# Taking the second chunk's edge counts in the lead-in, and moving list pieces behind the first chunk's norm

## The chip, the cores and the metric

The kernel runs as one program on one core of a Trainium2 chip. The metric is the device time of one execution in microseconds (us); with one core, the slowest core is that core. The engines are called by the names that the profile uses: PE (TensorE, matrix products), DVE (VectorE), ACT (ScalarE), POOL (GpSimd) and SP (SyncE, which only issues DMA transfers here). Each engine works through its own instructions in order.

## The reference, cut to what matters

Two layers run over 4096 tokens of width 256. In layer 0 a graph convolution is followed by a Mamba block and a mixture of experts; in layer 1 a second graph propagation, which keeps the 700 largest entries of each row, is followed by another mixture of experts.

```python
# layer 0, graph part, on x normalised
h = relu(adj @ x @ gcn_w + gcn_b)
h = layernorm(h) * ln_g + ln_b
... mamba(h): u = silu(conv(h @ w_in)); dt = softplus(...); scan over the 4096 tokens
# layer 1, graph part, on x normalised
sim  = tanh(adj * adj)
filt = sim * (adj > 0)
vals, idx = top_k(filt, 700)          # of each row
new_adj = filt with only these entries kept
feat = relu(new_adj @ (tanh(h @ W_proj + b_proj) @ W_gcn) + b_gcn)
```

The adjacency has few entries per row. If no row has more than 700 positive entries, the top-700 keeps everything, and `new_adj` is `filt`. The kernel counts the positive entries of each row to know that; were a row to have more, a branch at the end would compute the layer again.

## The kernel before, in words

The 4096 tokens are cut into 8 chunks of 512 (`CW`). Each chunk is a half-open range of rows of the adjacency; the kernel reads the transposed adjacency in tiles.

**The first propagation** (`propagation`, from L854) multiplies the adjacency with the normalised x. One chunk has two halves of 256 rows (`HW`), and one half has 8 tiles `at` (128 partitions x 4 x 256, 512 KB each, a pool of 3 buffers, loaded by SP at L795). A tile is used up in 4 pieces; one piece is one `yield` of the generator and two products at L871 (four records in the profile). After 32 pieces the half is copied out of PSUM by ACT (L877, tile `pts`), and a 33rd `yield` follows. Pieces are interleaved by hand with other work: `advance(k)` issues k of them. For chunk 0 the propagation is called with `count=True`: DVE then also adds up, tile by tile, which entries are positive (L864 for the first tile of a half, L866 for the others), into a bf16 tile `cnt`, which PE sums over partitions (L882) and DVE reduces to the largest row count (L886, L888, into `cmax`).

In what follows the 8 tiles of the first half of chunk 1 are called t0 to t7, and those of its second half s0 to s7.

**The lead-in** is what happens before the scan of chunk 0 can begin: chunk 0's propagation, then the steps 9 to 31 of `Front(0)`: bias and relu (L948, L952), statistics (L956 to L961), normalisation (`do_normal`, L964 on DVE and L968 on ACT), turning (L976), the in-projection (L999), convolution (L1016), `u`, `dt`, and the softplus of `dt` (`do_soft`, L1081 to L1089, in steps 28 to 31). Between these, the table `FILL` says how many pieces of chunk 1's propagation follow each step: 8 behind step 11, and so on up to all that are left for the lead-in behind step 26. The last 15 of the 66 pieces are issued in steps 0, 1, 2, 4 and 6 of the scan of chunk 0.

**Lists.** The rows of chunks 2, 4 and 6 are turned into lists of neighbours (`Lists.pair`, from L543), 128 rows pairwise at a time, so 6 pairs, of which 2 are done in the lead-in. One pair is 12 pieces on DVE: 8 that each scan a loaded 512 KB tile for the 8 largest of each segment (L577, L578; loads at L566), one that makes keys (L587 to L598), two that select (L606, L608), and one that finishes (L612 to L637). Before the change, 8 pieces run within the second half of chunk 0's propagation, the other 4 of the first pair directly behind chunk 0's last products, and all 12 of the second pair behind step 11.

**The scan** is 8 chunks of 32 steps. In each step DVE scans (two of L1377) and multiplies (L1387), ACT makes the decays (L1370), POOL makes the inputs (L1354) and starts an accumulating transfer (L1391). PE, DVE, ACT and POOL work in the order written by hand here; SP's order is left to the scheduler.

**The second propagation** (L1896 on) runs over the dense chunks 0, 1, 3, 5 and 7, 16 steps k of two blocks each. For each k, ACT makes tanh of the square of a tile `at1` (L1846 to L1848, three steps ahead), DVE counts its positive entries unless the chunk is 0 (L1853, L1856), PE multiplies (L1864); at the end of a chunk PE sums the counts (`total`, L1873), and DVE reduces them (L1878) and finishes the rows (`finish`, L1882, L1886). The rows of the listed chunks are gathered meanwhile: POOL starts one indirect transfer per list slot (L1726) into a ring of buffers, and DVE adds each in (L1742), 2.85 slots for each k. The manual order covers SP here too.

Of the kernel before, what the change touches and what calls it, by code (L numbers as in the profile page):

```python
# [10 lines left out]
F32 = mybir.dt.float32  # L11
BF16 = mybir.dt.bfloat16
I32 = mybir.dt.int32
AF = mybir.ActivationFunctionType
ALU = mybir.AluOpType
AX = mybir.AxisListType
# [3 lines left out]
P = 128  # L20
CW = 512
# [20 lines left out]
EARLY_LISTS = 12  # L42
# [4 lines left out]
def kernel(ctx: ExitStack, tc: tile.TileContext, out: bass.AP, **a):  # L47
    nc = tc.nc
# [3 lines left out]
    NT = N // P  # L52
# [730 lines left out]
    with ExitStack() as s1:  # L783
# [70 lines left out]
        def propagation(c, count=False):  # L854


            halves = psts[c] = []
            for r0 in range(c * CW, c * CW + CW, HW):
                pt = ps_pt.tile([P, DB, HW], F32, name="pt", tag="pt")
                for j4 in range(NT // 4):  # L860
                    at = ats.pop(0) if ats else adjacency(r0, j4)
                    if count and j4 == 0:
                        cnt = w2p.tile([P, 4, HW], BF16, name="cnt0", tag="db")
                        nc.vector.tensor_scalar(cnt, at, 0.0, None, ALU.is_gt)  # L864
                    elif count:
                        nc.vector.scalar_tensor_tensor(cnt, at, 0.0, cnt, ALU.is_gt, ALU.add)  # L866
                    for jj in range(4):
                        j = 4 * j4 + jj
                        for k in range(DB):

                            nc.tensor.matmul(  # L871
                                pt[:, k, :], xl[:, j, k * P:(k + 1) * P], at[:, jj, :],
                                start=(j == 0 and k == 0), stop=(j == NT - 1 and k == DB - 1),
                            )
                        yield
                pts = w1p.tile([P, DB, HW], F32, name="pts", bufs=2)
                nc.scalar.copy(pts, pt)  # L877
                halves.append(pts)
                if count:
                    pc = ps_y.tile([P, CW], F32, name="psy", tag="psy")  # L880
                    for jj in range(4):
                        nc.tensor.matmul(  # L882
                            pc[:1, :HW], ones[:, :1], cnt[:, jj, :], start=(jj == 0), stop=(jj == 3)
                        )
                    h = (r0 // HW) % 2
                    nc.vector.tensor_reduce(chalf[:, h:h + 1], pc[:1, :HW], AX.X, ALU.max)  # L886
                    if h == 1:
                        nc.vector.tensor_tensor(  # L888
                            cmax[:, c:c + 1], chalf[:, :1], chalf[:, 1:], ALU.max
                        )  # L890
                yield True
# [438 lines left out]
        class Step:  # L1330
# [64 lines left out]
            def total(self):  # L1395
                f, m = self.f, self.m
                if self.g == 0:
                    f.psy[m] = ps_y.tile([P, CW], F32, name="psy", tag="psy")
                    nc.tensor.matmul(
                        f.psy[m], dD[:, m, :], f.us[:, m, :], start=True, stop=False  # L1400
                    )
                last = 0 if self.paired else 1
                for j in range(last + 1):
                    nc.tensor.matmul(  # L1404
                        f.psy[m], ident, self.hc[:, j, :],
                        start=False, stop=(self.g == GS - 1 and j == last),
                    )
# [7 lines left out]
        with tc.manual_schedule(engines={  # L1415
# [19 lines left out]
            def advance(k=1, wait=False):  # L1435


                while k > 0:
                    k -= 1
                    if next(prop, None) and wait:  # L1440
                        break
                return k
# [41 lines left out]
                next(made)  # L1484
            advance(1)
            fr.do_gcn(1)
            for _ in range(EARLY_LISTS - NT // 4):
                next(made)
            prop, left = propagation(1), 2 * NT + 2 - late
            for i in range(9, STEPS):  # L1490
                fr.at(i, Front.EARLY)
                fr.at(i)
                if i == 11:
                    for _ in made:
                        pass
                k = min(FILL.get(i, 0), left)
                advance(k)
                left -= k
            advance(left)
            steps, tails, kept, gated, summed, owed = [], [], {}, [], 0, 0  # L1500
            for n in range(NC * STEPS):
                c, i = divmod(n, STEPS)
# [84 lines left out]
    with ExitStack() as s2:  # L1587
# [241 lines left out]
        cnts = {}  # L1829
# [12 lines left out]
        def source(k):  # L1842
            c, j2 = seq[k]
            at = ats.pop(k)
            f = ready[k] = wk.tile([P, 2, CW], F32, name="f1", bufs=LEAD + 1)
            nc.scalar.activation(f, at, AF.Relu)  # L1846
            nc.scalar.activation(f, f, AF.Square)
            nc.scalar.activation(f, f, AF.Tanh)  # L1848
            if c == 0:
                pass  # L1850
            elif j2 == 0:
                cnt = cnts[c] = tb.tile([P, 2, CW], BF16, name="cnt", bufs=2)
                nc.vector.tensor_scalar(cnt, at, 0.0, None, ALU.is_gt)  # L1853
            else:
                cnt = cnts[c]
                nc.vector.scalar_tensor_tensor(cnt, at, 0.0, cnt, ALU.is_gt, ALU.add)  # L1856
# [40 lines left out]
        with tc.manual_schedule(engines={  # L1897
            mybir.EngineType.PE, mybir.EngineType.DVE, mybir.EngineType.Activation,
            mybir.EngineType.Pool, mybir.EngineType.SP,
        }):  # L1900
            for k in range(AHEAD):
                fetch(k)
            for k in range(LEAD):
                source(k)
                fetch(k + AHEAD)
            features()
            taken.fetch()
            for k, (c, j2) in enumerate(seq):
                if k == TABLES:
                    table = table()  # L1910
                if j2 == 0:
                    pf = ps_f.tile([P, TPC, D], F32, name="pf")
                if k + LEAD < len(seq):
                    source(k + LEAD)
                if k + LEAD + AHEAD < len(seq):
                    fetch(k + LEAD + AHEAD)
                if ended is not None and k % H2 == 0:
                    finish(*ended)
                    ended = None
                if k in ROUTES:  # L1920
                    b = ROUTES[k]
                    routes[b] = route.prepare(b)
                for b in list(routes):
                    if next(routes[b], routes) is routes:
                        del routes[b]
                if k >= TABLES:
                    next(table, None)
                taken.upto(int(PACE * (k - 2)))
                product(k, pf)
                if j2 == H2 - 1:  # L1930
                    ended = (c, pf, total(c) if c else None)
            finish(*ended)
        assert not routes and taken.done == len(taken.slots)
        for _ in table:
# [239 lines left out]
```

## Time and profile before

| what | value |
|---|---|
| median of 6 runs | 2375.28 us (2367.64 to 2388.14) |
| the profiled execution | 2373.01 us |
| its span, first to last instruction | 2371.2 us |
| granted PE clock, mean | 0.942 |
| PE busy | 2103.5 us, 89% |
| DVE busy | 1812.9 us, 76% |
| ACT busy | 1193.4 us, 50% |
| POOL busy | 1401.2 us, 59% |
| counts of the second propagation (L1856) | 60 of 1.22 us |
| counts of chunk 0 in the first propagation (L866) | 14 of 1.21 us |

The span is that of one execution; 1.8 us of that execution's time lie outside it, and the median of the runs is 2.3 us above it. Busy shares are means over stages with different limits: lead-in 0 to 155 us, scan 155 to 1330 us, first experts up to about 1560 us, features of layer 1 to 1676 us, second propagation to 2069 us, last experts to the end.

In the rows of the timeline the columns are: start and duration in us, engine, line, operation, what it writes and reads, the shape, how many instructions are merged, and in brackets the idle time before it with what ended it. In the rows of windows they are: the window and its length, then each engine's busy time with its number of instructions (PE, its weight loads, DVE, ACT, POOL), the granted PE clock, the DMA engines' share and GB/s.

### The profile page before, as it was taken

How to read it: one execution, taken by the hardware profiler on the slowest of the kernel's cores; microseconds unless marked ns; L12 is line 12 of the kernel's file. 1: busy time of each engine (PE TensorE's matmuls, PEld its weight loads, DVE VectorE, ACT ScalarE, POOL GpSimd, SP SyncE). 2: the span in 40 equal slices, each digit the busy share in tenths (PEclk: the TensorE clock that was granted, in tenths of full speed). 3: DMA queues.
4: the chain of work that ended last, by engine and by line, in shares of the span. 5: the costliest groups of instructions: out<-in, count | busy, mean ns of one | idle time of the engine just before them, and what ended most of it. 6: DMA issues, size and time to landing. Idle time of an engine off the chain costs nothing. (4 is left out here: it accounts for less than half of the span.)

```text
span 2371.2 us, 28092 instructions
## 1 busy us (share of the span) xinstructions
PE 2103.5 (89%) x8235; PEld 1497.6 (63%) x8235; DVE 1812.9 (76%) x3207; ACT 1193.4 (50%) x2064; POOL 1401.2 (59%) x1056
## 2 busy tenths in 40 slices
PE   7899999999999999997896899968679799699884
PEld 6665565656665564654564787845568677577773
DVE  6959999999999999999997895145229799753242
ACT  4146657555665746567662223214368677333221
POOL 1037777787877778776762454420447677745551
PEclk9999999999999999998997999989879899899997
DMA  8559999999989999998975998734355555467794
GB/s 285 168 162 254 235 271 236 278 247 251 269 230 278 241 274 246 261 265 228 281 239 183 310 370 290 232 109 142 95 150 170 153 173 166 130 216 210 222 309 149
DMA packets 302677, 532.29 MB, mean 224 GB/s; under 512 B 31323, under 2 KB 170575, under 8 KB 301616
## 3 DMA queue, kind: packets, MB, share of 16 engines
q1 hardware_dynamic: 244720, 416.84, 55.2%
q0 software_dynamic: 57792, 113.54, 21.7%
q8 instruction: 69, 1.13, 0.2%
q14 instruction: 96, 0.79, 0.1%
HBM read 434.34 MB, written 49.02 MB: 204 GB/s over the span
## 5 line engine op out<-in xcount | busy, mean ns | idle before, releaser
L1354 POOL TENSOR_TENSOR db<-du,bb 128x1024 f32<-128x1024 f32 x256 | 607.5, 2373 | 312.7 <-DVE hc L1387 73.9
L1377 DVE TENSOR_TENSOR_SCAN db<-da,state,db 128x512 f32<-128x512 f32 x512 | 627.4, 1266 | 20.8 <-ACT da L1370 18.5
L871 PE MATMUL pt<-at,gn 128*128 128x256 f32 x2048 | 480.9, 388 | 19.4 <-ACT gn L129 9.7
L871 PEld LDWEIGHTS pt<-at,gn 128*128 128x128 f32 x2048 | 397.9, 195 | 141.8 <-issue 62.3
L1370 ACT ACTIVATE da<-dt,negA 128x512 f32<-128x512 f32 x512 | 346.1, 688 | 245.6 <-DVE db L1377 235.9
L1387 DVE TENSOR_TENSOR hc<-db,cb 128x1024 f32<-128x1024 f32 x256 | 327.6, 1280 | 17.9 <-issue 0.4
L1864 PE MATMUL pf<-gn,f 128*128 128x256 f32 x1280 | 297.2, 391 | 29.8 <-issue 27.3
L1864 PEld LDWEIGHTS pf<-gn,f 128*128 128x128 f32 x1280 | 249.7, 197 | 73.6 <-issue 39.8
L1404 PE MATMUL psy<-hc,ident 128*128 128x512 f32 x560 | 291.8, 614 | 2.9 <-DMA hc<-hc 2.9
L712 PE MATMUL ps_h<-xkT,wk 128*128 128x256 f32 x864 | 216.3, 392 | 21.0 <-DVE xkT L737 7.5
L697 PE MATMUL ps_y<-wk,hk 128*128 128x256 f32 x864 | 215.9, 385 | 7.1 <-issue 5.1
L702 DVE TENSOR_TENSOR yk<-ps_y,bk 128x512 f32<-128x512 f32 x73 | 50.2, 688 | 218.5 <-PE ps_y L697 170.8
L1391 POOL DMA_DIRECT2D hc<-hc x232 | 202.6, 873 | 0.2
L1726 POOL DMA_INDIRECT x<-gnd,ls_idx x128 | 157.1, 1227 | 74.2 <-issue 24.6
L712 PEld LDWEIGHTS ps_h<-xkT,wk 128*128 128x128 f32 x864 | 159.9, 194 | 60.6 <-ACT hk L716 14.4
L697 PEld LDWEIGHTS ps_y<-wk,hk 128*128 128x128 f32 x864 | 161.7, 192 | 29.8 <-issue 5.7
L1404 PEld LDWEIGHTS psy<-hc,ident 128*128 128x128 f32 x560 | 105.3, 194 | 83.2 <-issue 57.7
L1726 POOL DMA_INDIRECT ring<-gnd,ls_idx x88 | 107.2, 1219 | 56.5 <-DVE x L1742 36.2
L1846 ACT ACTIVATE f<-at 128x1024 f32<-128x1024 f32 x80 | 84.3, 1053 | 106.1 <-remote 63.8
L999 PE MATMUL ps_xz<-hT,w_in 128*128 128x512 f32 x256 | 117.0, 600 | 14.1 <-ACT hT L983 7.5
L716 ACT ACTIVATE hk<-ps_h,d0r_b 128x256 f32<-128x256 f32 x104 | 48.9, 474 | 136.4 <-PE ps_h L712 94.0
L1016 PE MATMUL ps_xz<-xc,dK 128*128 128x512 f32 x256 | 114.8, 592 | 0.0
(398 smaller groups left out, 2999.5 us busy)
## 6 DMA issues: line engine op xcount, KB each, us to landing
at<-in_adjT_dram SPq DMA_DIRECT2D x208, 512.0 KB
bb<-bcd SPq DMA_DIRECT2D x128, 512.0 KB
cb<-bcd SPq DMA_DIRECT2D x128, 512.0 KB
hc<-hc POOLq DMA_DIRECT2D x232, 256.0 KB
wk<-in_L_ffn_W_dram SPq DMA_DIRECT2D x70, 512.0 KB
wk<-in_L_ffn_expert_w_dram SPq DMA_DIRECT2D x114, 256.0 KB
ls_at<-in_adj_dram SPq DMA_DIRECT2D x32, 512.0 KB
hc<-in_adj_dram SPq DMA_DIRECT2D x16, 512.0 KB
```

What stands on the lines that cost most here:

```text
L697: nc.tensor.matmul(ps[:, j, :], hT[:, m, j * P:(j + 1) * P], w[:, m, :], start=(m == 0), stop=(m == kb_out - 1),)
L712: nc.tensor.matmul(ps[:, j, :], w[:, d, m * P:(m + 1) * P], xT[:, d, :], start=(d == 0), stop=(d == DB - 1),)
L871: nc.tensor.matmul(pt[:, k, :], xl[:, j, k * P:(k + 1) * P], at[:, jj, :], start=(j == 0 and k == 0), stop=(j == NT - 1 and k == DB - 1),)
L999: nc.tensor.matmul(ps, w_in[:, k, m * P:(m + 1) * P], self.hT[:, k, :], start=(k == 0), stop=(k == DB - 1),)
L1354: nc.gpsimd.tensor_tensor(self.db, self.f.du[self.half][:, self.mi:self.mi + 1, :].to_broadcast([P, 2, CW]), self.bb, ALU.mult,)
L1370: nc.scalar.activation(da, self.f.dt[self.half][:, self.mi, :], AF.Exp, scale=negA[:, self.m, n:n + 1])
L1377: nc.vector.tensor_tensor_scan(self.db[:, j, :], da, self.db[:, j, :], state[:, self.m, n:n + 1], ALU.mult, ALU.add,)
L1387: nc.vector.tensor_tensor(self.hc, self.db, self.cb, ALU.mult)
L1391: nc.gpsimd.dma_start(self.hc[:, 0, :], self.hc[:, 1, :], accum_op=ALU.add)
L1404: nc.tensor.matmul(f.psy[m], ident, self.hc[:, j, :], start=False, stop=(self.g == GS - 1 and j == last),)
L1726: nc.gpsimd.indirect_dma_start(out=to[:, :], out_offset=None, in_=gnd[:, :], in_offset=bass.IndirectOffsetOnAxis(ap=lists.idx[:, q, s:s + ...
L1864: nc.tensor.matmul(pf[:, t, :], f[:, jj, t * P:(t + 1) * P], gn[:, j, :], start=(j == 0 and t % 2 == 0), stop=(j == NT - 1 and t % 2 == 1),)
```

## The change

It edits four places.

- The 4 list pieces that stood behind chunk 0's last products are no longer issued there, and the second pair no longer in one go behind step 11. All 16 follow from step 11 on: one behind step 11, two behind each of steps 12 and 13, one behind each of steps 14 to 24.
- Chunk 1's propagation is called with `count=True`. Its two halves have a `cnt` tile each, in a third buffer of the tags `du` and `dt`, which chunk 0's `dt` and `du` use too. Both are summed at the end of the second half, in the accumulator's own PSUM bank (`pt`), by 8 products, and reduced by one instruction straight into `cmax`.
- The second propagation counts only the dense chunks 3, 5 and 7 (`c < 2` counts nothing).
- Its `total` and the reduction in `finish` are left out for chunk 1 as well.

```diff
-            halves = psts[c] = []
+            halves, cnts = psts.setdefault(c, []), []
...
                     if count and j4 == 0:
-                        cnt = w2p.tile([P, 4, HW], BF16, name="cnt0", tag="db")
+                        h = (r0 // HW) % 2
+                        tag = {"tag": "db"} if c == 0 else {"tag": ("du", "dt")[h], "bufs": 3}
+                        cnt = w2p.tile([P, 4, HW], BF16, name="cnt0", **tag)
+                        cnts.append(cnt)
...
-                if count:
-                    pc = ps_y.tile([P, CW], F32, name="psy", tag="psy")
-                    for jj in range(4):
...
+                if count and (c == 0 or len(cnts) == 2):
+                    pc = (ps_y if c == 0 else ps_pt).tile(
+                        [P, CW], F32, name="pc0", tag="psy" if c == 0 else "pt"
+                    )
+                    n, h = len(cnts), (r0 // HW) % 2 + 1 - len(cnts)
+                    for i, cnt in enumerate(cnts):
+                        for jj in range(4):
+                            nc.tensor.matmul(
+                                pc[:1, i * HW:(i + 1) * HW], ones[:, :1], cnt[:, jj, :],
+                                start=(jj == 0), stop=(jj == 3),
+                            )
+                    cnts.clear()
+                    nc.vector.tensor_reduce(
+                        (chalf if n == 1 else cmax)[:, (h if n == 1 else c):][:, :1],
+                        pc[:1, :n * HW], AX.X, ALU.max,
+                    )
...
             fr.do_gcn(1)
-            for _ in range(EARLY_LISTS - NT // 4):
-                next(made)
-            prop, left = propagation(1), 2 * NT + 2 - late
+            prop, left = propagation(1, True), 2 * NT + 2 - late
             for i in range(9, STEPS):
                 fr.at(i, Front.EARLY)
                 fr.at(i)
                 if i == 11:
-                    for _ in made:
-                        pass
+                    next(made)
+                elif i > 11:
+                    for _ in range(2 if i < 14 else 1):
+                        next(made, None)
                 k = min(FILL.get(i, 0), left)
                 advance(k)
...
-            if c == 0:
+            if c < 2:
                 pass
...
-                    ended = (c, pf, total(c) if c else None)
+                    ended = (c, pf, total(c) if c > 1 else None)
```

## The prediction

> **What bounds the kernel now.** I read windows by stage first, then the timelines of the lead-in, of the scan's first steps, and of chunk 1 in the second propagation. The chain of waits names no line above 6%, so the stages are taken one at a time.
>
> ```profile
> 0.00:155.00 155.00, 134.28 (x524) 100.40 (x525) 105.03 (x320) 53.89 (x97) 10.97 (x24) 0.97 0.63 206
> 155.00:1330.00 1175.00, 1091.09 (x3754) 687.88 (x3753) 1117.11 (x1199) 696.23 (x1327) 848.19 (x526) 0.96 0.92 252
> 1771.00:2069.00 298.00, 258.41 (x1188) 216.07 (x1186) 260.67 (x670) 205.09 (x214) 221.03 (x177) 0.94 0.53 157
> ```
>
> In the lead-in PE is nearly full and DVE has 50 us to spare. In the scan DVE is busy 1117.1 of 1175 us: whatever delays DVE there delays the end, whatever lies on others is hidden. In the second propagation from the end of chunk 0 (1771) on, DVE (87%) and PE (87%) share the bound.
>
> **Lead-in: what is taken off the path.** DVE and PE around chunk 0's norm:
>
> ```profile
> 77.58 0.21 DVE L587 TENSOR_SCALAR hc<-hc 128x128 f32<-128x128 f32 x1
> ...
> 86.03 1.28 DVE L948 TENSOR_TENSOR h<-ps_gcn,gcn_b 128x512 f32<-128x512 f32 x2
> ...
> 91.06 0.16 DVE L964 SCALAR_TENSOR_TENSOR ln_nm<-ln_mv,ln_rs 128x4 f32<-128x4 f32 x1 [1.21 <-POOL ln_rs L961]
> ```
> ```profile
> 78.31 7.93 PE L871 MATMUL pt<-at,gn 128*128 128x256 f32 x36
> 91.97 2.80 PE L976 MATMUL ps_turn<-ident,h 128*128 128x128 f32 x8 [5.74 <-ACT h L968]
> 94.57 5.33 PE L871 MATMUL pt<-at,gn 128*128 128x256 f32 x16
> ```
> ```profile
> 92.00:96.00 4.00, 3.95 (x12) 2.80 (x13) 3.93 (x8) 3.04 (x6) 0.00 (x0) 0.50 0.24 42
> ```
>
> The four list pieces hold DVE from 77.58 to 86.03. PE delivers chunk 0's last product at 78.46, so without them the bias starts 7.5 us sooner, the shift (L964) comes at 83 instead of 91.06, and ACT's normalisation (2.07 us) is over at 85.3, before PE runs out of pieces at 86.24. PE's gap of 5.74 us goes. So does what follows the gap: the granted clock is 0.50, eight turns take 2.80 us (1.04 at full clock, row at 1864.50) and 16 products 5.33 (3.62, row at 1785.55). That is 1.76 + 1.71 = 3.5 us, and PE's gain is **9.2 us**, call it 9.1 since hand-overs remain. From there PE is continuous up to 137.7, so the gain is carried. The Trainium skill, page "TensorE: Matmul & The Clock Gate", section "What's actually happening", has half the clock after an idle window of some 3.4 us and full clock again after as long a busy one; by it a cold window loses 1.7 us and PE's gain would be 7.4, where the rows lose 3.5.
>
> The 16 moved pieces cost 8.45 us for the pair's rest (77.58 to 86.03) and 29.4 for the second pair (91.14 to 120.5). They and the 13 counts that fall in the lead-in (13 x 1.14 us of pitch = 14.8) run from 83 on. The last piece stands behind step 24 and I place its end near 129.5; DVE was idle 24.45 us before the softplus, which is the cover. Eight loads of list tiles move with them in SP's queue; a tile `at` is released now by its count as well, but t0's count (85.6) still lets t3 land at 89, just before PE needs it. These I take at nothing; without the cover each late load would cost PE up to 3.4 us.
>
> **Lead-in: what is put on the path.** The counts stand in DVE's queue where their pieces are issued. Behind step 26 there are 24 pieces, up to the 51st: t7 and s0 to s4. The softplus stands behind them, and behind it the first input of the scan (POOL) and everything on DVE.
>
> ```profile
> 146.50 2.36 DVE L1081 SCALAR_TENSOR_TENSOR t<-t,du 128x1024 f32<-128x1024 f32 x2 [24.45 <-ACT t L1071]
> 149.81 2.36 DVE L1085 TENSOR_TENSOR du<-du,t 128x1024 f32<-128x1024 f32 x2 [0.95 <-ACT du L1075]
> ```
> ```profile
> 152.77 0.37 SPq L795 DMA_DIRECT2D at<-in_adjT_dram  x1
> ```
>
> The row at 152.77 is the load of s4: three buffers, so it waits until PE has used s1. Its bytes move until 156.1, 3.4 us. PE being 9.1 us ahead, s4 is issued at 143.7, lands at 147.1, is counted by 148.3; then L1081 for 2.3 us, and L1085 at 150.6 against 149.81. ACT's logarithm, 9.1 us early, no longer ends last. So of the 9.1 us nothing is left: **+0.8 us**. Ends: -9.1, if DVE reached the softplus as early as ACT allows; and if PE gained nothing, s4 would be counted at 152.77 + 3.4 + 1.14 = 157.3 and L1085 start at 159.6: +9.8.
>
> **First steps of the scan.** s5, s6 and s7 are counted in steps 0, 2 and 4: 3 x 1.14 = +3.4 us on a full DVE. At the end of step 6 the reduction waits for PE's last piece, ACT's copy and 8 products.
>
> ```profile
> 183.28 1.23 DVE L1387 TENSOR_TENSOR hc<-db,cb 128x1024 f32<-128x1024 f32 x1
> 184.42 2.45 DVE L1377 TENSOR_TENSOR_SCAN db<-da,state,db 128x512 f32<-128x512 f32 x2
> ...
> 189.18 2.46 DVE L1377 TENSOR_TENSOR_SCAN db<-da,state,db 128x512 f32<-128x512 f32 x2 [0.99 <-ACT da L1370]
> ...
> 195.11 2.46 DVE L1377 TENSOR_TENSOR_SCAN db<-da,state,db 128x512 f32<-128x512 f32 x2 [1.79 <-ACT da L1370]
> ```
> ```profile
> 185.97 1.89 PE L871 MATMUL pt<-at,gn 128*128 128x256 f32 x8
> ```
>
> DVE is through step 6 at 184.42, PE through the last piece at 187.86: 3.4 us late. Copy 0.6, products 1.1 (four took 0.60), reduction 0.7: DVE would stand for 5.9 us if PE keeps that distance, 2.4 if the counts let PE catch up. I take 4.2. Of it 0.99 + 1.79 = 2.8 come back, since DVE waited for ACT in the next steps anyway. Sum 3.4 + 4.2 - 2.8 = **+4.8 us**, ends +3.0 and +9.3 (nothing comes back).
>
> **Second propagation.** 15 counts of 1.14, one of 0.60, one reduction of 0.60 leave DVE: 18.3 us. Four of them ran before 1771, where DVE idled for 34.5 us.
>
> ```profile
> 1829.88 0.59 PE L1873 MATMUL pc<-cnt,ones_b 128*1 128x512 bf16 x2
> ```
> ```profile
> 1838.14 0.67 DVE L1878 TENSOR_REDUCE cmax<-pc 1x1 f32<-1x512 f32 x1
> 1838.74 1.27 DVE L1882 TENSOR_TENSOR x<-pf,b_gcn_b 128x512 f32<-128x512 f32 x2
> ```
> ```profile
> 1774.28 1.12 POOL L1726 DMA_INDIRECT x<-gnd,ls_idx  x1 [2.50 <-DVE x L1742]
> ```
>
> PE is through chunk 1 at 1829.9; DVE finishes it at 1838.74, busy without a pause for 10 us. Relieved of 14.3 us between 1771 and there, DVE comes to meet PE, not more: 1838.74 - 1829.9 = **-8.8 us**, which I carry to the end, since DVE leads in chunks 3 to 7. Ends: PE's own slack in the chunk is 2.7 us (395 products of 0.2155 and its other work make 88.6 of 91.3), so -11.5; and if POOL's gathers lead, they gain only the three pauses for DVE at 1774 to 1785 (2.50, 1.74, 2.30, less 0.30 that each issue takes): -5.6.
>
> **Sum** on the execution's own span: 2371.2 + 0.8 + 4.8 - 8.8 = 2368.0; 1.8 lie outside the span and the median is 2.3 above that execution: **2372.1 us**. Ends: -9.1 + 3.0 - 11.5 = -17.6, or 2357.7; 9.8 + 9.3 - 5.6 = +13.5, or 2388.8.
>
> **Rivals.**
> - *DVE's relief is worth all of itself.* Between 1838 and 1864 PE waited for ACT 2.75 and 8.49 us, ACT for loads that a late count held; if a DVE that arrives on time ends these too, all 18.3 us count: 0.8 + 4.8 - 18.3 = -12.7, **2362.6**. Against: PE was through chunk 1 at 1829.9 already.
> - *Counts as waits for PE* (slower). In the lead-in and at step 6 DVE stands behind work of PE. If PE does not come earlier (list loads before t4 in SP's queue, clock gate elsewhere), s4 is late, nothing comes back at step 6: +13.5, **2388.8**. It passes zero where PE keeps less than 5.9 of its 9.1 us. For it: SP's order is the scheduler's. Against: PE's only gap there is the one removed.
> - *Gathers keep the second propagation's time*: POOL issued without a pause from 1787 to 1850. 0.8 + 4.8 - 0 = +5.6, **2380.9**.
>
> **How the numbers follow.** 0.5% is 11.9 us; less can hardly be told from no change. Forecast 0.40 (2366 to 2380 by itself), relief 0.25, counts as waits 0.27, gathers 0.08. Faster by over 0.5%: the relief, 0.25. Slower: 0.27 and a third of the gathers, 0.30. Same: 0.45. The range takes in both ends: 2358 to 2389.
>
> **What would show it.** The turn (L976) with no gap and at full clock, near 86; L1081 released by a count near 148, not by ACT; three counts between scans and a reduction with a wait of some 4 us at step 6; DVE's finish of chunk 1 within 2 us of PE's last product of it. The forecast is wrong if the softplus starts before 143, if a load holds PE between 90 and 137, or if chunk 1 keeps its length. The spell of PE at clock 0.50 from 1697 to 1735 (27.3 us without a releaser) I leave as it is; were it tied to what the gathers do, all this would be small beside it.

## The result, and the profile after

The changed kernel takes 2395.17 us, median of 20 runs (2382.91 to 2402.63), against 2374.61 us (2359.48 to 2390.41, 46 runs): a ratio of 1.0082, 95% interval 1.0066 to 1.0097. It is slower by some 20 us, where 3 us less was forecast. The profiled execution took 2393.91 us with a span of 2392.0 (2371.2 before), at a granted clock of 0.941 (0.942 before). In the changed file the lines of the propagation stand 3 further down, those of the front and the scan 11, those of the second propagation 12.

In the lead-in the timeline of PE shows what was announced: no gap before the turn, full clock in and after it (rows as in the prediction: start, duration, engine, line, names, and in brackets the idle time before).

```profile
86.75 1.04 PE L987 MATMUL ps_turn<-ident,h 128*128 128x128 f32 x8
87.63 3.63 PE L874 MATMUL pt<-at,gn 128*128 128x256 f32 x16
```

The timeline of DVE in the changed kernel, at the end of the lead-in and in the first steps of the scan:

```profile
147.98 1.23 DVE L869 SCALAR_TENSOR_TENSOR cnt<-at,cnt 128x1024 bf16<-128x1024 f32 x1 [2.25 <-DMA at<-in_adjT_dram]
149.12 2.35 DVE L1092 SCALAR_TENSOR_TENSOR t<-t,du 128x1024 f32<-128x1024 f32 x2
151.46 2.36 DVE L1096 TENSOR_TENSOR du<-du,t 128x1024 f32<-128x1024 f32 x2
...
160.61 2.46 DVE L1388 TENSOR_TENSOR_SCAN db<-da,state,db 128x512 f32<-128x512 f32 x2 [2.24 <-POOL db L1365]
...
196.00 0.68 DVE L894 TENSOR_REDUCE cmax<-pc 1x1 f32<-1x512 f32 x1 [6.43 <-PE pc L889]
196.60 2.44 DVE L1388 TENSOR_TENSOR_SCAN db<-da,state,db 128x512 f32<-128x512 f32 x2
199.08 1.23 DVE L1398 TENSOR_TENSOR hc<-db,cb 128x1024 f32<-128x1024 f32 x1
200.22 2.45 DVE L1388 TENSOR_TENSOR_SCAN db<-da,state,db 128x512 f32<-128x512 f32 x2
...
204.64 2.46 DVE L1388 TENSOR_TENSOR_SCAN db<-da,state,db 128x512 f32<-128x512 f32 x2 [0.71 <-ACT da L1381]
```

The softplus (L1092) stands behind a count that waits for the load of s4, and its second input (L1096) starts at 151.46 where the kernel before had 149.81: 1.65 us later. Step 9 of the scan starts at 204.64 against 195.11 before: 9.5 us later. The rest of the loss is in the second propagation. The windows by stage, with the same columns as in the prediction; the second one's edges are moved with the scan, and the last runs from chunk 0's finish to chunk 7's:

```profile
0.00:156.65 156.65, 141.40 (x571) 107.59 (x572) 119.26 (x333) 53.93 (x97) 10.97 (x24) 0.99 0.67 214
156.65:1341.00 1184.35, 1082.26 (x3725) 678.75 (x3724) 1122.96 (x1205) 697.21 (x1329) 851.89 (x526) 0.96 0.91 249
...
1790.40:2092.10 301.70, 263.25 (x1185) 216.41 (x1184) 246.33 (x656) 205.08 (x215) 213.35 (x176) 0.93 0.52 154
```

In the last row DVE has 14.3 us less to do than before (246.33 against 260.67), as foreseen, and yet the stretch is longer than before's 298.0. The whole account, one execution against one:

| stretch | before | after | difference |
|---|---|---|---|
| start of the first scan | 158.96 | 160.61 | +1.65 |
| from there to step 9 of the scan | 36.15 | 44.03 | +7.9 |
| from there to the second propagation's first product | 1481.7 | 1483.2 | +1.5 |
| its products, first to last | 380.9 | 394.9 | +14.0 |
| from there to the end | 313.5 | 309.3 | -4.2 |

Within the products, chunk 0's finish comes 94.3 us after the first product before and 102.5 after; chunk 1 takes 67.6 us before and 77.2 after; chunk 3 81.5 and 77.9; chunks 5 and 7 differ by 0.0 and 1.5. What chunks 1 and 3 take varies by itself: with chunk 1's counts in their place, e2, f1 and g1 below take 76.9, 77.0 and 77.6 us for chunk 1 and 75.0, 75.6 and 73.2 for chunk 3, so the 67.6 and 81.5 are that one execution's. Chunk 0's finish is the firmer mark: 91.1 and 91.5 us in e2 and g1.

**Where PE stands.** In the table of waits of PE (waiting tile and line, releaser; us in total, times, longest) the wait without a releaser in the second propagation has grown. The kernel before, then the changed one:

```profile
PE pf L1864 <- issue: 27.3, 15, 2.5
```
```profile
PE pf L1876 <- issue: 45.2, 41, 2.2
```

This is the slow spell that the prediction left as it was. Before, it begins after 1698 and ends by 1738.6; in the changed kernel it runs from 1711.6 to 1762.5, and comes back from 1830.8 to 1842.2. Its rows in PE's timeline, before and after:

```profile
1676.81 21.32 PE L1864 MATMUL pf<-gn,f 128*128 128x256 f32 x98
...
1707.63 0.59 PE L1864 MATMUL pf<-gn,f 128*128 128x256 f32 x1 [2.23 <-issue]
1710.42 0.58 PE L1864 MATMUL pf<-gn,f 128*128 128x256 f32 x1 [2.20 <-issue]
...
1738.56 41.74 PE L1864 MATMUL pf<-gn,f 128*128 128x256 f32 x182 [0.22 <-issue]
```
```profile
1699.73 11.02 PE L1876 MATMUL pf<-gn,f 128*128 128x256 f32 x49
...
1742.21 0.58 PE L1876 MATMUL pf<-gn,f 128*128 128x256 f32 x1 [1.54 <-issue]
1744.99 0.58 PE L1876 MATMUL pf<-gn,f 128*128 128x256 f32 x1 [2.20 <-issue]
...
1762.49 37.81 PE L1876 MATMUL pf<-gn,f 128*128 128x256 f32 x163 [0.60 <-issue]
```

A row of one product every 2 to 2.8 us, then 182 or 163 in one go. What ends the spell is seen on POOL, in the last row of the first burst of gathers and the first row after it, before and after:

```profile
1736.44 1.00 POOL L1726 DMA_INDIRECT x<-gnd,ls_idx  x1 [0.46 <-issue]
1757.35 1.13 POOL L1726 DMA_INDIRECT ring<-gnd,ls_idx  x1 [19.91 <-DVE x L1742]
```
```profile
1758.08 1.00 POOL L1738 DMA_INDIRECT x<-gnd,ls_idx  x1 [0.31 <-issue]
1793.63 1.12 POOL L1738 DMA_INDIRECT x<-gnd,ls_idx  x1 [34.54 <-DVE x L1754]
```

The first burst is 40 gathers before (from 1681.90) and 49 after (from 1692.93), mostly 1.30 to 1.31 us apart. POOL stops when no buffer is free, that is when DVE stops adding. And what stops DVE is, before, the first count of chunk 1, which waits for its tile's load; after, nothing until chunk 0's finish:

```profile
1755.99 0.69 DVE L1853 TENSOR_SCALAR cnt<-at 128x1024 bf16<-128x1024 f32 x1 [34.52 <-DMA at<-in_adjT_dram]
```
```profile
1790.41 1.29 DVE L1894 TENSOR_TENSOR x<-pf,b_gcn_b 128x512 f32<-128x512 f32 x2 [44.80 <-PE pf L1876]
```

So the theory to be tested: **the counts were a governor**. A count waits for a load, the load for a buffer, the buffer for ACT, ACT for PE; so a count in DVE's queue keeps the adds, and with them the gathers, near PE's own place. Without chunk 1's counts DVE adds as fast as gathers land, POOL gathers without a pause, and PE crawls while it does. Rivals: the spell varies by chance; the loss lies in the lead-in and the scan; the relief of DVE is worth what was forecast and something else costs more.

### The profile page after: what moved, and what is told of

Read it like the earlier page. It is cut to its first block, busy times and chain, and to the rows that moved or that the text cites. A ratio compares the mean times of both kernels' runs of the same rounds, so it can differ in the third digit from the quotient of the medians.

```text
span 2392.0 us, 28110 instructions
## 1 busy us (share of the span) xinstructions
PE 2108.4 (88%) x8241; PEld 1495.5 (63%) x8241; DVE 1813.9 (76%) x3207; ACT 1193.3 (50%) x2064; POOL 1396.4 (58%) x1056
## 5 line engine op out<-in xcount | busy, mean ns | idle before, releaser
L1876 PE MATMUL pf<-gn,f 128*128 128x256 f32 x1280 | 309.2, 397 | 47.3 <-issue 45.2
L1738 POOL DMA_INDIRECT x<-gnd,ls_idx x128 | 148.1, 1157 | 108.0 <-DVE x L1754 52.8
```

Of the source, the lines that this page charges most:

```text
L1738: nc.gpsimd.indirect_dma_start(out=to[:, :], out_offset=None, in_=gnd[:, :], in_offset=bass.IndirectOffsetOnAxis(ap=lists.idx[:, q, s:s + ...
L1876: nc.tensor.matmul(pf[:, t, :], f[:, jj, t * P:(t + 1) * P], gn[:, j, :], start=(j == 0 and t % 2 == 0), stop=(j == NT - 1 and t % 2 == 1),)
```

## The experiments

Ratios are to the kernel before in runs of the same session, with 95% intervals. Spans and starts are of one profiled execution each; two executions of the same stage differ by some microseconds, up to 10 in chunk 0 of the second propagation. The kernel before has medians from 2361.7 to 2379.0 us in these sessions, so whole times of different sessions are compared by their ratios alone.

### Each part alone, and the counts' hold without their work

**e1**: the kernel before, without chunk 1's counts and sum.

```diff
-            if c == 0:
+            if c < 2:
                 pass
...
-                    ended = (c, pf, total(c) if c else None)
+                    ended = (c, pf, total(c) if c > 1 else None)
```

> The kernel before, with chunk 1's counts and their sum left out of the second propagation and nothing else (chunk 1's count is left out of the computation; its entry of cmax is set to 0). Theory, the counts as a governor: a count waits for the load of its tile, and the load waits for ACT and PE, so the counts hold DVE, and with it the release of the list buffers, to PE's pace. Without them POOL issues gathers in longer unbroken bursts, and PE crawls while they last: products from the first to the last of the second propagation 381 us before, 391 to 397 here, PE's idle time put down to issue at that line 67 us before, 95 to 115 here; ratio 1.004 to 1.006. Rival, the relief as predicted: chunk 1's finish comes 8.8 us earlier, ratio 0.996. Rival, chance: the spell varies by itself; ratio 0.998 to 1.002.

Measured: 1.0049 (1.0021 to 1.0078). The first burst is 49 gathers, as in the changed kernel; chunk 0's finish comes 100.7 us after the first product, chunk 1 takes 76.0 us (94.3 and 67.6 before). In the view that the expectation used, which adds weight loads, issue accounts for 81.4 us (67.1 before, 95 to 115 expected); the products take 385.4 us from first to last, less than the 391 expected. Neither that wait nor chunk 1's length tells the kernels apart: e2 and g1 below, which count as before, have 86.0 and 87.3 us of issue, and chunk 1 at 76.9 and 77.6. The burst does (40 gathers in both), and chunk 0's finish (91.1 and 91.5), and the products (379.7 in both). The ratio and its sign are the governor's: work is taken away from DVE, nothing is added but one memset of `cmax` at the start, and the kernel is slower. Of the 0.0049 (12 us) this profile places some 5 us, in the products; where the rest lies isn't shown.

**e2**: the kernel before, with the list pieces moved as in the change, nothing counted in the lead-in.

> The kernel before, with only the 16 list pieces moved behind chunk 0's norm, nothing counted in the lead-in. If the lead-in's gain is worth what the prediction worked out for its bound: the turn has no gap, PE 9 us earlier from there, no count in front of the softplus, which is released by ACT near 138; first scan 8 to 9 us earlier, kept through the scan; ratio 0.9962 to 0.997. Rival: DVE reaches the softplus no earlier, since the moved pieces stand there, or the gain is lost in the first steps: ratio 0.999 to 1.001.

Measured: 0.9952 (0.9927 to 0.9978), 11 us less, a little more than expected; its profile is of an execution 9.6 us above its median. DVE's timeline: the softplus waits for ACT alone, and the first scan is 10 us earlier than before.

```profile
136.52 2.36 DVE L1081 SCALAR_TENSOR_TENSOR t<-t,du 128x1024 f32<-128x1024 f32 x2 [14.98 <-ACT t L1071]
...
148.97 2.46 DVE L1377 TENSOR_TENSOR_SCAN db<-da,state,db 128x512 f32<-128x512 f32 x2 [2.24 <-POOL db L1354]
```

At step 9, 7.1 us of the 10 are left (188.0 against 195.1), since DVE waits there for ACT. So one half of the change is a gain by itself, and the counts spend it.

**e3** and **e4**: the changed kernel, with a copy of one column where the count stood, for chunk 1's tiles (e3) and for chunk 0's too (e4, `c < 2`).

```diff
-            if c < 2:
+            if c == 1:
+                tie = tb.tile([P, 1], F32, name="tie", bufs=2)
+                nc.vector.tensor_copy(tie, at[:, 0, :1])
+            elif c < 2:
                 pass
```

> The changed kernel, with one copy of 128x1 elements on DVE for each tile of chunk 1 in the second propagation, at the place where the count stood and waiting for the same load. Governor: DVE is held to PE's pace again at some 0.1 us a tile instead of 1.2; first burst about 40 gathers again (49 after), chunk 0's finish 8 us earlier against the start of the second propagation, chunk 1 from 77 back to 68 us or less; the time 14 to 20 us below the changed kernel's, ratio to the kernel before 1.000 to 1.003. Rivals (relief of work, chance, or the loss lies in the scan): 1.007 to 1.009 as the changed kernel.

> As the one before, with the copy for the tiles of chunk 0 as well. Governor: DVE is held from the first tile on, so the first burst is shorter than before's 40 gathers, 30 to 36, and PE's slow spell in chunk 0 (some 37 us beyond its work before, 45 after) shrinks by 1.3 us for each gather less, 5 to 13 us: ratio to the kernel before 0.994 to 1.000. Rivals: as the changed kernel, 1.007 to 1.009; or, if DVE held earlier makes the loads later, worse than the one before.

Measured: e3 1.0008 (0.9982 to 1.0034), e4 0.9996 (0.9971 to 1.0021). Against the changed kernel's 1.0082 that is 17.6 and 20 us, for instructions that do nothing but wait. The view of the tile `tie` in e4 (first row: count, shortest/median/longest duration in ns; then who ended its waits, us and times):

```profile
L1863 DVE COPY tie<-at x32: 143/148/155, 1470.9 to 1823.6; 128x1 f32<-128x1 f32 x32
...
  DMA at<-in_adjT_dram: 69.2, 11
```

0.15 us of work each, and 69.2 us of waiting. The first burst is 40 gathers in e3 and 26 in e4 (49 after); chunk 0's finish comes at 84.5 and 82.7 us (102.5), chunk 1 takes 73.9 and 70.8 (77.2), issue is 20.0 and 16.3 us (45.2), the products 367.2 and 361.7 us (394.9). Chunk 1 gets to neither before's 67.6 nor the 68 expected. Chunk 3 takes 71.0 and 70.8 us (81.5 before), but e1, which has no hold, has 71.0 as well, so that isn't the hold's. The products as a whole sort the kernels: without counts or copies for chunk 1 385.4 to 394.9 us (e1, g4, the changed kernel), with counts 379.7 to 380.9 (before, e2, g1), with copies alone 361.7 to 373.4 (e3, e4, f3, f4).

### The lead-in and the first steps

**f3**: e4 with the reduction of chunk 1's count behind step 9 of the scan.

```diff
+                if n == 9:
+                    nc.vector.tensor_reduce(cmax[:, 1:2], held.pop()[:1], AX.X, ALU.max)
```

> As e4 (the changed kernel with both copies), with the reduction of chunk 1's count moved from the end of step 6 of the scan to the end of step 9; PE's products for it stay. The prediction's step for the scan: the wait for PE (6.43 us measured, 4.2 foreseen) goes. If the wait is what sets step 9: step 9's scan, at 203.7 in e4, starts at 198 to 200; ratio 0.997 to 0.9985. If ACT or PE are late at steps 7 to 9 anyway (they were in e2, where DVE waited 3.83 and 1.79 us for da): 202 to 203.5, ratio as e4, 0.9990 to 1.0005.

Measured: 0.9987 (0.9967 to 1.0007), which covers e4's value. DVE's timeline at steps 7, 8 and 9 of f3:

```profile
189.58 2.45 DVE L1392 TENSOR_TENSOR_SCAN db<-da,state,db 128x512 f32<-128x512 f32 x2
...
195.28 2.46 DVE L1392 TENSOR_TENSOR_SCAN db<-da,state,db 128x512 f32<-128x512 f32 x2 [1.93 <-ACT da L1385]
...
201.21 2.46 DVE L1392 TENSOR_TENSOR_SCAN db<-da,state,db 128x512 f32<-128x512 f32 x2 [1.80 <-ACT da L1385]
```

Step 7 is 6.1 us earlier than in e4 (195.66), step 9 only 2.5 (203.69): the wait for the reduction is gone, and waits for ACT take most of its place. Of the two readings offered neither is met; the truth lies between.

**f4**: e4 with the list pieces back where the kernel before has them.

> As e4, with the list pieces where the kernel before has them, so that only the counts are new in the lead-in. The prediction's bound for a PE that gains nothing: the load of s4 at 152.8, counted at 157.3, the second input of the softplus at 159.6 and the first scan at 168 to 169 (160.2 in e4, 159.0 in before): ratio to the kernel before 1.002 to 1.004, e4's plus 8 to 9 us. Rival: the counts cost the same without the moved pieces, first scan at 160 to 162, ratio 0.999 to 1.001.

Measured: 1.0168 (1.0120 to 1.0216), four times the excess expected; the first scan starts at 197.9. PE's timeline in the lead-in:

```profile
93.75 3.37 PE L874 MATMUL pt<-at,gn 128*128 128x256 f32 x12
125.75 2.07 PE L874 MATMUL pt<-at,gn 128*128 128x256 f32 x4 [28.63 <-DMA at<-in_adjT_dram]
```

The 12 pieces of the second pair run on DVE in one go, the counts of chunk 1 stand behind them, a tile `at` isn't released until it is counted, and PE stands for 28.63 us for a load that cannot start. Spreading the pieces is what makes the counts bearable in the lead-in at all; the prediction's worst case for late counts (+9.8) was far too small for this order.

**f1**: e2 with the copies for chunk 0 (chunk 1's counts stay where they were).

> The kernel before with the list pieces moved (as in e2) and the one-column copy for the tiles of chunk 0 in the second propagation; chunk 1's counts stay in the second propagation as before. Governor: the lead-in's 8 us of e2 stay, and DVE is held from the first tile, so the first burst is 26 to 32 gathers (40 in e2) and chunk 0's finish comes 80 to 85 us after the first product of the second propagation (91 in e2): 6 to 10 us less than e2, ratio 0.990 to 0.993. Rival, the counts' work matters and not the holding: as e2, 0.995; or the two gains take each other's place: 0.994 to 0.997.

Measured: 0.9948 (0.9916 to 0.9979). Chunk 0's finish comes at 78.8 us, just under the 80 to 85 expected (91.1 in e2), and the burst is 26 gathers, but the ratio is e2's: the 12 us by which these two executions differ there do not show in the time. Against e4, which has the same hold and the lists moved too, f1 says what it costs to count chunk 1 early, less what its counts cost in the second propagation: 0.9996 - 0.9948 = 0.0048, some 11 us for the worse. At step 9 e4 is 17.1 us behind f1 (203.7 against 186.6).

### Is it the gathers' pace?

The pause is a memset of 128x8 on POOL behind each of the first gathers:

```diff
                         bounds_check=N - 1, oob_is_err=False,
                     )
+                    if self.next <= 60:
+                        for _ in range(4):
+                            nc.gpsimd.memset(pause, 0.0)
```

**f2** is f1 with four of them behind 60 gathers, **g1** the kernel before with one behind 40, **g4** the changed kernel with one behind 80, **h1** and **h2** the kernel before with two and four behind 40.

> As f1, with four memsets of 128x8 on POOL behind each of the first 60 gathers, so that gathers follow at 1.7 to 1.8 us instead of 1.30. If PE's slow spell comes from gathers issued at POOL's full pace: PE's idle time put down to issue at its products of the second propagation falls below 8 us (30 to 35 in before and e2), chunk 0's finish at 62 to 75 us after the first product; ratio 0.984 to 0.990. If only the number of gathers in a row matters and not their pace: the spell lasts longer, since the same gathers take longer; ratio 0.995 to 1.000. If POOL becomes the bound: ratio 0.993 to 0.998 with no spell.

> The kernel before with one memset of 128x8 on POOL behind each of the first 40 gathers, nothing else: pitch 1.6 to 1.8 us in place of 1.30. If POOL's pace makes PE's slow spell: PE's idle time put down to issue at the products of the second propagation below 8 us (29.8 before), chunk 0's last product 60 to 70 us after the first (94 before); then DVE's adds are behind and PE waits for them at the first routing, 10 to 25 us; ratio 0.990 to 1.000. If the pace makes no difference: a spell of 35 us or more, ratio 1.000 to 1.008.

> The changed kernel with the pause of g1 behind each of its first 80 gathers and no copies. If the loss in the second propagation is PE's crawling under gathers at full pace: issue idle below 10 us (47.3 after), the second propagation's products 395 us from first to last there, 370 to 385 here; ratio 0.999 to 1.004. If DVE has to be held for other reasons: 1.007 or more.

> The kernel before with two memsets of 128x8 on POOL behind each of the first 40 gathers: one fits into the gap of 0.30 us, the second adds to the pitch, 1.31 to about 1.6 us. If the pace makes the spell and 1.4 to 1.5 us is what a gather takes further down (later gathers follow at 1.48 us on average without a spell): issue idle below 10 us (29.8 before), chunk 0's last product 60 to 70 us after the first (94 before), then PE waits for DVE at the first routing; ratio 0.990 to 1.000. If the number in a row makes it, at any pace: a spell of 35 to 45 us, ratio 1.000 to 1.006.

> The same with four memsets, pitch 2.25 us. Pace: no spell, chunk 0's products in 57 to 62 us as in f2, and then the adds are late by 25 to 35 us, since 40 of them at 2.25 us take 90 us; ratio 1.003 to 1.012. Number: a spell of 60 us or more; ratio 1.010 to 1.020.

In g1 and g4 the pause has no effect: one memset fits into the 0.30 us that pass between two gathers anyway, and the pitch stays 1.31. The spell stays too (34.8 us of idle time before PE's products in g1, 39.0 in g4). Their ratios, 1.0007 (0.9985 to 1.0029) and 1.0056 (1.0031 to 1.0080), say nothing on the pace. In h1 the pitch is 1.9 to 2.0 us in most gaps, more than the 1.6 aimed at. POOL's and PE's timelines in h1:

```profile
1702.94 1.01 POOL L1726 DMA_INDIRECT x<-gnd,ls_idx  x1 [0.64 <-issue]
1703.95 0.28 POOL L1733 MEMSET pause<- 128x8 f32 x2
1704.87 1.01 POOL L1726 DMA_INDIRECT x<-gnd,ls_idx  x1 [0.64 <-issue]
```
```profile
1682.34 65.78 PE L1868 MATMUL pf<-gn,f 128*128 128x256 f32 x304
...
1778.59 2.36 PE L144 MATMUL ps_tr<-ident,xn_r 128*128 128x128 f32 x8 [19.52 <-DVE xn_r L134]
```

304 products in one go, through an unbroken run of gathers: **the spell comes from gathers at POOL's full pace, not from their number alone**; chunk 0's products are done in 55 us (94 before). In f2 and h2, mostly at 2.2 to 2.3 us, step 16 is reached after the same time. At full pace the length of the first burst sets the spell's: chunk 0's finish comes at 68.7 to 72.1 us behind 22 gathers (g3, h3, i1, i2 below), 78.8 to 83.5 behind 26 (e4, f1, f3), 84.5 to 94.3 behind 40 (before, e2, e3, g1) and 100.5 to 102.5 behind 49 (after, e1, g4). This order leaves little room for chance as the reason for chunk 0's length; within one length of burst it varies by up to 10 us. But the time doesn't fall: h1 1.0001 (0.9965 to 1.0036), h2 1.0025 (0.9993 to 1.0058), f2 1.0087 (1.0055 to 1.0118), worse than any of its three readings. Fewer slots are in, DVE's adds stand ahead of the first routing in its queue, and PE waits there for `xn_r`, 19.52 us in h1 and 25.70 in f2. What PE gains by not crawling it gives back waiting for the gathers.

What ACT does in the spell, and the DMA queues, show how far the spell reaches. The kernel before; step 8 of ACT is the first tile in the spell:

```profile
1730.79 1.06 ACT L1846 ACTIVATE f<-at 128x1024 f32<-128x1024 f32 x1 [34.15 <-remote]
```

The table of queues (packets, MB, share of 16 engines) from 1712 to 1736, before and in h1:

```profile
q0 software_dynamic: 768, 1.47, 21.2%
q1 hardware_dynamic: 272, 0.52, 7.4%
```
```profile
q1 hardware_dynamic: 1360, 2.62, 36.7%
q0 software_dynamic: 576, 0.09, 2.6%
```

q0 carries the gathers, q1 SP's loads. Before, these 24 us see one load of a tile's 512 KB, in h1 five. That is not because loads are slow there: SP issues only one. Its six loads before that one were issued by 1694.85 and all their packets had moved by 1698.0; the next is issued at 1731.87, when ACT has read a tile and freed its buffer, and has moved by 1735.2, with gathers still running. ACT is what is late. Its tile for step 8 was there at 1688.6, and the buffer that it writes is free when PE's step 4 is done; the record of that step's last product ends at 1694.24, but the signal of it, by the trace's semaphore events, comes at 1730.77. In h1 each of the first 20 such signals comes within 0.1 us of its product's end. So in the spell PE's word reaches ACT late, ACT's tiles are late, and SP's loads with them: the links of the theory, ACT for PE and the load for ACT, are there. Whether only the signal is late or the product too, whose end in a record is modelled, the trace doesn't tell.

### Asking for the slots more slowly

DVE adds 2.85 slots for each step. **g3** is f1 with 2 in each of the first 20 steps and 3.1 after; **g2** the same without copies and with one memset behind 40 gathers; **h3** has 2 for 12 steps and 3.5 after; **h4** adds two memsets behind 30 gathers; **i1** has 2 for 8 steps and 3.15 after; **i2** is g3 with the routings of chunks 2 and 4 later. In g2 and g3 the routing of these two chunks reads rows whose last slots aren't added yet, so they compute something else and only their stages count.

```diff
-                taken.upto(int(PACE * (k - 2)))
+                taken.upto(2 * (k - 2) if k < 10 else 16 + int(3.15 * (k - 10)))
```

> As e2 (list pieces moved), with the pause of g1 and fewer list slots asked for in the first 22 steps of the second propagation (2 for each step, 3.1 after, in place of 2.85 throughout), so that DVE isn't behind at the first routing. No spell, no wait there: chunk 0 at 58 to 66 us (91 in e2), up to 25 us less than e2, some given back where 3.1 slots a step are too many: ratio 0.984 to 0.991. If POOL is the bound of the whole: as e2, 0.995.

> As f1 (list pieces moved, one-column copies for chunk 0), with the slots asked for as in g2 and no pause. Fewer gathers are asked for early, but they come at POOL's full pace: the first burst 20 to 24 gathers (26 in f1), chunk 0 at 70 to 78 us (78.8 in f1), issue idle 12 to 22 us; ratio 0.990 to 0.994.

> As f1 (list pieces moved, one-column copies for chunk 0), with 2 slots asked for in each of the first 12 steps that ask for any, and 3.5 in each one after. No pause. The first burst is 20 to 24 gathers (26 in f1), chunk 0's finish at 68 to 76 us after the first product (78.8 in f1), issue idle 10 to 20 us; ratio 0.987 to 0.992. If the steeper demand later brings the spell back: as f1, 0.993 to 0.996.

> As h3, with two memsets behind each of the first 30 gathers (pitch about 1.6). Pace: no spell in chunk 0, its finish at 58 to 66 us; 30 gathers at 1.6 us are issued by 53 us, so nothing is late at the first routing; ratio 0.982 to 0.988. Number: as h3 or up to 9 us more, 0.990 to 0.996.

> As f1 (list pieces moved, one-column copies for chunk 0), with 2 slots asked for in each of the first 8 steps that ask for any and 3.15 after, between f1's 2.85 throughout and h3's 2 and 3.5. If late gathers at the routings are the other side of the loss: chunks 3 and 5 at 74 to 80 us (89.7 and 86.6 in h3, 75.6 and 74.5 in f1), chunk 0 at 72 to 78, ratio 0.992 to 0.998. If h3's loss was something else: as h3, 1.002.

> As g3 (2 slots in each of the first 20 steps, then 3.1), with the routing of chunk 2 from step 37 on in place of 29 and that of chunk 4 from 57 in place of 55, so that each stands behind its last slots. If the routings' place is what costs: the products of the second propagation in 355 to 365 us (380.9 before, 369.2 in f1), ratio 0.985 to 0.991. If the bound is the gathers' own pace: 368 to 380 us, 0.993 to 1.000.

| kernel | ratio | interval | chunk 0's finish | chunks 1, 3, 5, 7 |
|---|---|---|---|---|
| g2 | 0.9933 | 0.9908 to 0.9957 | 83.7 | 70.9, 71.2, 81.2, 81.5 |
| g3 | 0.9876 | 0.9836 to 0.9916 | 69.4 | 71.0, 71.1, 82.9, 76.3 |
| h3 | 1.0024 | 0.9992 to 1.0055 | 68.7 | 78.0, 89.7, 86.6, 72.8 |
| h4 | 1.0031 | 0.9997 to 1.0064 | 62.2 | 87.3, 85.3, 87.6, 73.3 |
| i1 | 0.9896 | 0.9867 to 0.9924 | 72.1 | 77.5, 74.1, 91.6, 68.4 |
| i2 | 0.9935 | 0.9913 to 0.9957 | 71.5 | 65.0, 83.4, 82.8, 87.3 |

Chunk 0's finish comes where it was expected in h3, h4 and i1, and within 0.6 us of it in g3; not in g2, whose memset is the one that fits the gap. The times do not follow. In h3 and h4 (0.987 to 0.992 and 0.982 to 0.988 expected) later chunks take 85 to 90 us, which fits slots that are asked for faster than they come in; no run shows it by itself. i2's products take 388.3 us, outside both of its readings; its ratio lies in the second, in which the gathers' own pace is the bound. i1 is faster than both kernels, by 25 us against before, and better than was expected of it; its profile is of an execution 9 us above its median and still shows a spell in chunk 5 (91.6 us), so the profile doesn't tell where its gain over f1 is, nor, with 6 runs against f1's 10 in another session, how large it is. That stays open.

## Why the prediction was wrong

- **Lead-in, +0.8 us: right.** 1.65 measured. Gap and half clock went as worked out, PE stayed ahead, s4 landed at 147.98 (147.1 foreseen), and the count put the softplus behind it. That PE's 9 us were real and were spent by the counts is shown by e2 (first scan 10.0 us earlier).
- **First steps, +4.8 us: the mechanism right, the size low.** 7.9 measured, inside the ends of 3.0 and 9.3. Three counts as foreseen; DVE stood 6.43 us for PE and reduced for 0.6, 7.0 instead of 4.2 and above that term's upper end of 5.9, as PE stood 5.86 us for ACT (`zs`) and ran at half clock behind it; and of the 2.8 us that were to come back, 2.1 did (DVE waits 0.71 for ACT where it waited 0.99 and 1.79). Part of the 7.9 is the execution before: e1, g1, h1 and h2, with the same first steps, take 36.0 to 38.9 us for them (36.15 before), and e3, e4 and g4, with the changed ones, 43.3 to 44.5. f3 shows the reduction's place is worth 6.1 us at step 7 and 2.5 at step 9.
- **Second propagation, -8.8 us: the step that failed.** The prediction said: "Relieved of 14.3 us between 1771 and there, DVE comes to meet PE, not more", and carried the gain to the end; its ends were -11.5 and -5.6. The products took 14.0 us more (8 to 9 in g4, 5 in e1). The relief was there (DVE 14.3 us less busy), but a count was not only work: its wait for a load held the gathers to PE's pace. e1 (slower by taking work away) and e3 (17.6 us regained by 16 copies of 0.15 us that only wait) show it. The sign named for this step missed too: DVE's finish of chunk 1 comes 6.0 us behind PE's last product of it, not within 2. The rows for it were in the page before: DVE idle for 34.52 us in front of a count was read as slack that could be left out of the sum, and it was the hold.
- **"The spell ... I leave as it is; were it tied to what the gathers do, all this would be small beside it."** It is tied to them (h1), and it was the largest term.
- **Rivals.** *Counts as waits for PE* has nearly the right number (2388.8 forecast, 2395 measured) for a wrong reason: PE kept its 9 us. Its mechanism is real in f4, where the lists stay in one go. *Gathers keep the second propagation's time* (0.08) named the right engine and priced it at nothing lost; the loss by it wasn't among the cases. *Relief is worth all*: not borne out, and under the same hold its worth can't be told: e4, f3 and f4, with copies alone, take 361.7, 373.4 and 367.6 us for the products, f1, with the same copies for chunk 0 and chunk 1's counts, 369.2.

## What to carry to other kernels

An instruction that waits is also a brake on everything behind it on its engine: before one is taken out, name what it holds back, and what that will run into when it runs free. Idle time of an engine in front of a wait is slack only if nothing downstream feeds on the engine's lateness. If a brake is what is needed, a wait costs 0.15 us of work, and need not be a 1.2 us count.

## What the runs showed of the hardware

- With gathers issued every 1.30 us PE starts a product mostly every 1.4 to 2.8 us, though its inputs are there (before, the next step's input was done at 1696.6). The first gaps come at a granted clock of 1.00 (1698 to 1702); from 1706 to 1738 it is 0.50. With pauses, at 1.9 to 2.0 or 2.2 to 2.3 us, PE runs 304 (h1, h2) and 256 (f2) products without a pause. ACT's instructions keep their 1.06 us. The Trainium skill, page "SBUF — State Buffer", section "Who interferes with whom", says that PE and ACT never wait on anyone, speaking of the ports of SBUF. For ACT the rows agree; PE's wait has no releaser in the trace, and these runs do not tell what it is for.
- In the same spell a signal of PE comes 36.5 us behind the record of the product that sends it (1730.77 and 1694.24, before), and within 0.1 us of it where the gathers are spaced out (h1). Loads that are issued in the midst of it move their 512 KB in 3.3 to 3.5 us (before, issued at 1731.87 and moved by 1735.2; in the changed kernel, issued at 1715.6 and 1738.4 and moved by 1719.2 and 1741.7): the hardware queue is short of loads to move, not held up.
- A memset of 0.12 us between two gathers costs nothing (pitch 1.30 to 1.31), a second one costs 0.6 to 0.7 us (1.9 to 2.0).
